# A state-space layer and a mixture of experts in one program: channel sums by column tiles of TensorE, and other ranks for the chain ahead of the next chunk's scan

## The chip, the cores and the metric

The kernel runs on one NeuronCore of a Trainium2 chip, in fp32. The metric is the device time of one execution in microseconds (us); lower is better. The core has five engines with a queue each: TensorE (PE, matmul; its weight loads are shown as PEld), VectorE (DVE), ScalarE (ACT), GpSimd (POOL) and SyncE (SP), whose queue issues nearly all of the DMAs here. Each queue is worked off in the order in which the kernel issued it.

## The reference

The input x has 8 images of 384 channels and 32 x 32 pixels; a sequence has 1024 tokens. Two layers follow each other, each added to its own input.

```python
# layer 0, on _gn(x): a selective state-space block
mu = t.mean(-1, keepdims=True); var = t.var(-1, keepdims=True)         # over the 384 channels
t = (t - mu) * rsqrt(var + 1e-05) * ln_w + ln_b
xm, z = split(t @ in_proj_w.T)                                         # 768 channels each
xc = silu(conv over 3 tokens (xm) + conv_b)
dt, Bm, Cm = split(xc @ x_proj_w.T, [24, 24 + 16])                     # 768 -> 56 channels
dt = softplus(dt @ dt_proj_w.T + dt_proj_b)
hst = exp(dt * A) * hst + dt * xc * Bm;  y = sum_n hst * Cm            # a scan over tokens, 16 states
t = ((y + xc * D) * silu(z)) @ out_proj_w.T
t = gelu(t @ mlp_w1.T + mlp_b1) @ mlp_w2.T + mlp_b2
# layer 1, on _gn(x): 4 experts, the two best weighted for each pixel
```

`_gn` is a group norm in 32 groups of 12 channels. The two products that the change is about are the means over 384 channels (mean and variance) and `xc @ x_proj_w.T`.

## The kernel before

**Tiling.** Channels lie on the 128 partitions, tokens on the free axis. A chunk is 512 tokens of one image (`NCH` = 16 chunks); the 384 channels make `J` = 3 tiles, the 768 inner channels `ND` = 6. The 16 states stand as 4 on the partitions and `NG` = 4 groups. A chunk so has 6 x 4 = 24 **rounds**, one for each inner tile and group, 384 in all.

**A round** (the main loop from L1008) is written out by hand: the sum over states of the last round (`sum_states`, four 32-column products y, L776), two pairs of scans on VectorE (L750), the drive of the next round on GpSimd (du, L742, 128x2048), the decays on ScalarE (da_A and da_B, L734), and the product with C, half on VectorE and half on GpSimd (L754). The tiles are few: three du, one da_A, one da_B, one y.

**The side work** is done between these. It is a set of Python generators (tasks); each yields before a step the engine that it needs, the planner's cost in us, and a least wait in slots. A round has three slots (`side`), in each of which TensorE gets 2.7 us of credit, VectorE 0.6 and ScalarE 2.7, 1.8 or 0.7. `issue` takes the tasks in order of urgency, which is

```python
return self.rank * PATIENCE + self.ready
```

with `PATIENCE` = 6 slots, so a lower rank goes first. The default rank is 2. "bank" stands for TensorE with a PSUM bank out of four (`ps_g`), "batch" for a SiLU or GELU batch that brings its own table loads on ScalarE. `plan(i, k)` says which tasks begin in round k of chunk i: `gate`, `conv` and `silus` for the next chunk n = i + 1, then `x_proj(n)` at k = 11, `delta(n, 0)` and `delta(n, 1)` at k = 17 and 21, `norm(n + 1)` at k = 21. Four lanes run throughout: output projection, hidden MLP layer, second MLP layer, and the first expert layer, which keeps up with the chunks. All this is settled when the program is built, so the order on each engine is fixed.

**What the change touches.** `norm` computes the mean of the three channel tiles as three products with a full 128x128 matrix of 1/384, accumulated in one PSUM bank mu (L266), so that each partition holds the mean; VectorE subtracts it (L268); ScalarE squares (sq, L275); three more products give var (L279), followed by Ln and Exp (L281, L283), a VectorE product (L285) and the affine step (L289). The weights of the mean carry the group norm's scale (mean_w, L253). `x_proj` accumulates six products with 56 columns in g_x (L360), one for each inner tile as its SiLU is done, and ScalarE copies the 56 rows to dbc (L365). Its B and C rows go to DRAM and come back spread over partitions (L368, L373). `delta` makes dt from dbc: product g_dt (L398), three ScalarE steps (L402 to L406), VectorE (L408), then dtx = dt * xc on GpSimd (L411), DMAs of both to DRAM and back, repeated over partitions (L384, L390). `statistics` reads x in parts (L241) for the group norm, from SP's queue, in a buffer of its own (`pst`). `seed` starts y with the skip term D * xc; the very first one is a product with the matrix skip (L767).

The router's logits already have the form that the change gives to the others: three 32-column products side by side (L577), a copy (L581), products that add the parts (L584).

After the scans come the last chunk's projections and MLP, the remaining expert hidden products (L622), the routing, and the second expert layer (L944).

Of the kernel before, what the change touches and what calls it, by code (L numbers as in the profile page):

```python
# [11 lines left out]
F32 = mybir.dt.float32  # L12
AF = mybir.ActivationFunctionType
ALU = mybir.AluOpType
# [4 lines left out]
P = 128  # L19
# [91 lines left out]
def layers(ctx, tc, io, ident, cmean, eps, dram, x1_dram, gn1, logits, r_dram, group_norm):  # L111
# [9 lines left out]
    def pool(name, bufs, stack=ctx, **kw):  # L121
# [7 lines left out]
                              for name, bufs in (("p1", 1), ("pdt", 2), ("pxt", NH), ("pdu", 3), ("psq", 2)))  # L129
    pz, pxc, ph, pbc, pst = (pool(name, bufs, scanning)  # L130
                             for name, bufs in (("pz", ND), ("pxc", 2 * ND), ("ph", HID), ("pbc", NG), ("pst", 1)))
# [23 lines left out]
    w_x = weight("x_proj", [P, ND, DTR + 2 * NS])  # L155
# [11 lines left out]
    V.tensor_reduce(sum_j, ident[0:32 * J, 0:32 * J].rearrange("p (j m) -> p m j", j=J)[:, 0:E, :], AX.X, ALU.add)  # L167
    e_b1 = weight("e_b1", [P, E * J])
# [12 lines left out]
    skip = wp.tile([P, P], F32, name="skip")  # L181
    V.tensor_scalar(skip, ident, d_skip[:, 0:1], None, ALU.mult)
# [49 lines left out]
    def statistics(b):  # L232
        st = p2.tile([P, NH * J, 6], F32, name="st")
        for k in range(NH):
            for j in range(J):
                if b == 0:
                    part = xt[k][:, j, :]
                else:
                    yield "-", 0, 3
                    part = pst.tile([P, T], F32, name="part")  # L240
# [11 lines left out]
        mean_w = p1.tile([P, P], F32, name="mean_w")  # L252
        S.activation(mean_w, cmean, AF.Identity, scale=g[:, 0:1])  # L253
        S.activation(g[:, 1:2], small[:, 0:1], AF.Identity, bias=g[:, 1:2], scale=-float(J))
        free()
        gn[b] = g, mean_w

    def norm(i):
# [4 lines left out]
        yield "bank", 3, 0  # L263
        mu = bank("mu")
        for j in range(J):
            PE.matmul(mu, lhsT=mean_w, rhs=x[:, j, :], start=(j == 0), stop=(j == J - 1))  # L266
# [3 lines left out]
        sq, var = [], None  # L270
        for j in range(J + 1):
            if j < J:
                yield "ACT", 0.65, 2 * (j == 0)
                sq.append(psq.tile([P, T], F32, name="sq"))
                S.activation(sq[j], x[:, j, :], AF.Square, bias=g[:, 1:2])  # L275
            if j > 0:
                yield "PE" if var else "bank", 1, 1
                var = var or bank("var")
                PE.matmul(var, lhsT=cmean, rhs=sq[j - 1], start=(j == 1), stop=(j == J))  # L279
# [72 lines left out]
    def x_proj(i):  # L352
        g = None
        m = DTR + 2 * NS
        for d in range(ND):
            while (i, d) not in xc:
                yield "-", 0, 1
            yield "bank" if d == 0 else "PE", 1, 1 if d % 3 == 0 else 0
            g = bank("g_x") if d == 0 else g
            PE.matmul(g[0:m, :], lhsT=w_x[:, d, :], rhs=xc[i, d], start=(d == 0), stop=(d == ND - 1))  # L360
# [724 lines left out]
```

## Time and profile before

| | |
|---|---|
| Median of 3 runs | 3993.1 us (3990.06 to 3995.06) |
| Profiled execution | 3992.75 us |
| Its span, first to last instruction | 3990.6 us, mean granted TensorE clock 0.96 |
| First scan, last round's first scan | 77.2 us, 3296.4 us from the start |
| Mean round | 8.4 us |
| TensorE busy | 3663.8 us (92%) |
| GpSimd, VectorE, ScalarE busy | 2776.9, 3031.7, 2421.2 us |
| mu (L266), var (L279), g_x (L360): busy | 47.6, 53.4, 91.7 us |

All views come from the one profiled execution. A line of a group or timeline gives the source line, the engine, the operation, what it writes and reads, and how many there are; an fp32 matmul stands as two records. A line of the waits view reads "engine, line waited for: us in total, times, longest". The timeline gives start, length, and in brackets the idle time of the engine before it and what ended it. Matmuls are pipelined, so their length is longer than what they occupy: the start of the next tells that.

### The profile page before, as it was taken

How to read it: one execution, taken by the hardware profiler on the slowest of the kernel's cores; microseconds unless marked ns; L12 is line 12 of the kernel's file. 1: busy time of each engine (PE TensorE's matmuls, PEld its weight loads, DVE VectorE, ACT ScalarE, POOL GpSimd, SP SyncE). 2: the span in 40 equal slices, each digit the busy share in tenths (PEclk: the TensorE clock that was granted, in tenths of full speed). 3: DMA queues.
4: the chain of work that ended last, by engine and by line, in shares of the span. 5: the costliest groups of instructions: out<-in, count | busy, mean ns of one | idle time of the engine just before them, and what ended most of it. 6: DMA issues, size and time to landing. Idle time of an engine off the chain costs nothing.

```text
span 3990.6 us, 35138 instructions
## 1 busy us (share of the span) xinstructions
PE 3663.8 (92%) x10294; PEld 1381.3 (35%) x10294; DVE 3031.7 (76%) x3081; ACT 2421.2 (61%) x3762; POOL 2776.9 (70%) x1070
## 2 busy tenths in 40 slices
PE   6679898899999999999999999999999889899999
PEld 2213233333333333333333333333333334344444
DVE  3898999888888887788888887888787881255554
ACT  4658677767687768676777777777767663200000
POOL 2898999788888888788878888888788880000000
PEclk8879899999999999999999999999999999999999
DMA  4344444465545454555455454555554443555553
GB/s 131 128 143 147 157 147 163 138 206 171 177 147 194 164 186 141 199 175 183 156 171 200 162 173 152 196 173 169 165 181 163 163 161 101 205 210 182 194 188 106
DMA packets 372499, 665.31 MB, mean 167 GB/s; under 512 B 40252, under 2 KB 151228, under 8 KB 370132
## 3 DMA queue, kind: packets, MB, share of 16 engines
q1 hardware_dynamic: 342496, 612.38, 46.2%
q10 hardware_dynamic: 29812, 50.68, 3.4%
q8 instruction: 83, 1.36, 0.1%
q14 instruction: 108, 0.88, 0.1%
HBM read 535.90 MB, written 127.01 MB: 166 GB/s over the span
## 4 chain that ended last, share of the span: by engine, by line
PE 51%; ACT 24%; DVE 13%; DMA 5%; issue 4%; POOL 2%; SPq 1%; ACTq 0%; DVEq 0%; POOLq 0%
PE acc L944 12%; PE acc L521 7%; PE e_hid L622 6%; PE hid L482 6%; PE g_in L297 5%; PE g_out L460 5%; ACT da_A L734 5%; PE y L776 5%; DVE da_A L750 4%; DVE du L750 4%; ACT da_B L734 3%; ACT L193 2%; PE g_dt L398 2%; ACT h L497 2%; DVE du L754 1%
## 5 line engine op out<-in xcount | busy, mean ns | idle before, releaser
L742 POOL TENSOR_TENSOR du<-dxr,b 128x2048 f32<-128x2048 f32 x384 | 1739.0, 4529 | 33.6 <-PE y L776 22.0
L754 POOL TENSOR_TENSOR du<-du,c 128x1024 f32<-128x1024 f32 x384 | 905.6, 2358 | 146.3 <-DVE du L750 127.4
L734 ACT ACTIVATE da_B<-dtr_b,w_a_log 128x512 f32<-128x512 f32 x768 | 527.3, 687 | 358.8 <-DVE du L750 321.6
L734 ACT ACTIVATE da_A<-dtr_a,w_a_log 128x512 f32<-128x512 f32 x768 | 528.3, 688 | 268.8 <-DVE carry L759 126.5
L776 PE MATMUL y<-du,sel 128*32 128x512 f32 x3072 | 467.1, 634 | 133.1 <-DVE du L754 65.3
L297 PE MATMUL g_in<-xt,in_proj 128*128 128x512 f32 x1152 | 566.6, 631 | 19.9 <-ACT edge L314 5.6
L482 PE MATMUL hid<-tt,mlp_w 128*128 128x512 f32 x1152 | 536.7, 609 | 45.9 <-ACT h L486 45.5
L750 DVE TENSOR_TENSOR_SCAN du<-da_B,carry,du 128x512 f32<-128x512 f32 x384 | 488.4, 1272 | 94.9 <-ACT da_B L734 93.5
L521 PE MATMUL acc<-h,mlp_w 128*128 128x512 f32 x1152 | 532.5, 605 | 19.3 <-ACT h L497 6.8
L750 DVE TENSOR_TENSOR_SCAN du<-da_B,du 128x512 f32<-128x512 f32 x384 | 465.0, 1211 | 95.2 <-ACT da_B L734 72.7
L622 PE MATMUL e_hid<-xn,e_w 128*128 128x512 f32 x1080 | 504.9, 615 | 26.9 <-ACT r L626 11.0
L750 DVE TENSOR_TENSOR_SCAN da_A<-da_A,carry,du 128x512 f32<-128x512 f32 x384 | 490.2, 1277 | 36.0 <-ACT da_A L734 35.9
L944 PE MATMUL acc<-r,w_e_w 128*128 128x512 f32 x1152 | 494.6, 592 | 0.0
L750 DVE TENSOR_TENSOR_SCAN da_A<-da_A,du 128x512 f32<-128x512 f32 x384 | 466.4, 1215 | 25.3 <-ACT da_A L734 23.5
L754 DVE TENSOR_TENSOR du<-da_A,c 128x1024 f32<-128x1024 f32 x384 | 470.3, 1225 | 13.2
L297 PEld LDWEIGHTS g_in<-xt,in_proj 128*128 128x128 f32 x1152 | 214.1, 197 | 369.9 <-issue 266.7
L482 PEld LDWEIGHTS hid<-tt,mlp_w 128*128 128x128 f32 x1152 | 218.0, 193 | 340.9 <-issue 254.3
L521 PEld LDWEIGHTS acc<-h,mlp_w 128*128 128x128 f32 x1152 | 214.5, 192 | 327.2 <-issue 253.8
L944 PEld LDWEIGHTS acc<-r,w_e_w 128*128 128x128 f32 x1152 | 218.9, 190 | 275.5 <-issue 275.5
L622 PEld LDWEIGHTS e_hid<-xn,e_w 128*128 128x128 f32 x1080 | 204.4, 195 | 316.5 <-issue 247.3
L411 POOL TENSOR_TENSOR dtx<-dt,xc 128x512 f32<-128x512 f32 x96 | 121.9, 1269 | 271.9 <-DVE dt L408 256.4
L460 PE MATMUL g_out<-xc,out_proj 128*128 128x512 f32 x576 | 271.6, 620 | 14.8 <-DVE xc L783 11.0
(129 smaller groups left out, 3021.3 us busy)
## 6 DMA issues: line engine op xcount, KB each, us to landing
dxr<-dxr_dram SPq DMA_DIRECT2D x384, 256.0 KB, 4.6
mlp_w<-in_mlp_w SPq DMA_DIRECT2D x384, 192.0 KB, 2.7
dtr_b<-dtr_dram SPq DMA_DIRECT2D x192, 256.0 KB, 4.2
dtr_a<-dtr_dram SPq DMA_DIRECT2D x192, 256.0 KB, 3.2
r_dram<-r ACTq DMA_DIRECT2D x192, 256.0 KB, 3.3
r<-r_dram SPq DMA_DIRECT2D x64, 768.0 KB, 4.6
in_proj<-in_in_proj SPq DMA_DIRECT2D x192, 192.0 KB, 3.5
e_w<-in_e_w SPq DMA_DIRECT2D x192, 192.0 KB, 2.6
```

The lines of the kernel that those rows point to most:

```text
L297: PE.matmul(g, lhsT=w[:, j, :], rhs=xt[i][:, j, :], start=(j == 0), stop=(j == J - 1))
L411: G.tensor_tensor(dtx, dt, xc[i, d], ALU.mult)
L460: PE.matmul(g, lhsT=w[:, d, :], rhs=xc[i, 3 * k + d], start=(k + d == 0), stop=(k == 1 and d == 2))
L482: PE.matmul(g, lhsT=w[:, j, :], rhs=tt[i][:, j, :], start=(j == 0), stop=(j == J - 1))
L521: PE.matmul(g, lhsT=w[:, n, :], rhs=hs[mine[n]], start=(k + n == 0), stop=(k == 1 and n == 2))
L622: PE.matmul(h, lhsT=w[:, j, :], rhs=xn[:, j, :], start=(j == 0), stop=(j == J - 1))
L734: S.activation(out, dtr[i, d][pair][:, j % 2, :], AF.Exp, scale=neg_a[:, d, j, s:s + 1])
L742: G.tensor_tensor(du[r], dxr[i, d], wide(bt[i, s].unsqueeze(1), [P, Q, T]), ALU.mult)
L750: V.tensor_tensor_scan(a if j < 2 else b, a, b, start, ALU.mult, ALU.add)
L754: engine.tensor_tensor(du[r][:, js, :], h, wide(ct[i, s].unsqueeze(1), [P, 2, T]), ALU.mult)
L776: PE.matmul(y[j * m:(j + 1) * m, :], lhsT=sel, rhs=h[:, j, :], start=False, stop=(s == NG - 1), tile_position=(0, j * m), skip_group_check ...
L944: PE.matmul(acc[j], lhsT=e2[:, e, d, j, :], rhs=r[:, d, :], start=(e + d == 0), stop=(e + d == E + J - 2))
```

## The change

Mean and variance: each of the three channel tiles goes to its own 32 columns of TensorE (`tile_position`) and so to its own 32 partitions of the PSUM bank. ScalarE copies these 96 rows into a psq tile, and one product with a 96x128 matrix of 1/32 adds them and spreads the sum over all partitions, into the same bank. The variance's products come after all three squares, not one after each. `x_proj`: the weights are padded with zeros to 64 columns, two inner tiles go side by side, three times; ScalarE copies the 128 rows, and one product with a matrix of two stacked unit matrices adds the halves. The parts for `statistics`, the copies and skip share the pool psq with the squares (three buffers in place of two, and `pst` is gone). Ranks: `conv` 2 to 1, the SiLU of xc and `x_proj` 2 to 0, `norm` 2 to 1 and begun at k = 18 in place of 21. Planner's costs follow.

```diff
-                              for name, bufs in (("p1", 1), ("pdt", 2), ("pxt", NH), ("pdu", 3), ("psq", 2)))
+                              for name, bufs in (("p1", 1), ("pdt", 2), ("pxt", NH), ("pdu", 3), ("psq", 3)))
...
-    w_x = weight("x_proj", [P, ND, DTR + 2 * NS])
+    w_x = wp.tile([P, ND, 64], F32, name="w_x_proj")
+    G.memset(w_x, 0.0)
+    S.dma_start(w_x[:, :, 0:DTR + 2 * NS], io["x_proj"])
+    sum_x = wp.tile([P, DTR + 2 * NS], F32, name="sum_x")
+    V.tensor_tensor(sum_x, ident[:, 0:DTR + 2 * NS], ident[:, 64:64 + DTR + 2 * NS], ALU.add)
...
+    spread = wp.tile([32 * J, P], F32, name="spread_j")
+    G.memset(spread, 1.0 / 32)
...
-                    part = pst.tile([P, T], F32, name="part")
+                    part = psq.tile([P, T], F32, name="sq")
...
-        mean_w = p1.tile([P, P], F32, name="mean_w")
-        S.activation(mean_w, cmean, AF.Identity, scale=g[:, 0:1])
+        mean_w = p1.tile([P, 32], F32, name="mean_w")
+        S.activation(mean_w, cmean[:, 0:32], AF.Identity, scale=g[:, 0:1])
...
+    def over_channels(out, weights, parts):
+        for j in range(J):
+            PE.matmul(out[32 * j:32 * (j + 1), :], lhsT=weights, rhs=parts[j], start=True, stop=True,
+                      tile_position=(0, 32 * j))
+        yield "ACT", 0.6, 2
+        rows = psq.tile([P, T], F32, name="sq")[0:32 * J, :]
+        S.copy(rows, out[0:32 * J, :])
+        yield "PE", 1, 2
+        PE.matmul(out, lhsT=spread, rhs=rows, start=True, stop=True)
...
-        yield "bank", 3, 0
+        yield "bank", 1.2, 0
         mu = bank("mu")
-        for j in range(J):
-            PE.matmul(mu, lhsT=mean_w, rhs=x[:, j, :], start=(j == 0), stop=(j == J - 1))
+        yield from over_channels(mu, mean_w, [x[:, j, :] for j in range(J)])
...
-        sq, var = [], None
-        for j in range(J + 1):
-            if j < J:
-                yield "ACT", 0.65, 2 * (j == 0)
-                sq.append(psq.tile([P, T], F32, name="sq"))
-                S.activation(sq[j], x[:, j, :], AF.Square, bias=g[:, 1:2])
-            if j > 0:
-                yield "PE" if var else "bank", 1, 1
-                var = var or bank("var")
-                PE.matmul(var, lhsT=cmean, rhs=sq[j - 1], start=(j == 1), stop=(j == J))
+        sq = []
+        for j in range(J):
+            yield "ACT", 0.65, 2 * (j == 0)
+            sq.append(psq.tile([P, T], F32, name="sq"))
+            S.activation(sq[j], x[:, j, :], AF.Square, bias=g[:, 1:2])
+        yield "bank", 1.2, 2
+        var = bank("var")
+        yield from over_channels(var, cmean[:, 0:32], sq)
...
-        for d in range(ND):
-            while (i, d) not in xc:
+        for d in range(0, ND, 2):
+            while (i, d) not in xc or (i, d + 1) not in xc:
                 yield "-", 0, 1
-            yield "bank" if d == 0 else "PE", 1, 1 if d % 3 == 0 else 0
-            g = bank("g_x") if d == 0 else g
-            PE.matmul(g[0:m, :], lhsT=w_x[:, d, :], rhs=xc[i, d], start=(d == 0), stop=(d == ND - 1))
+            yield "bank" if d == 0 else "PE", 1.1, 1 if d != 2 else 0
+            if d == 0:
+                g = bank("g_x")
+            for k in range(2):
+                PE.matmul(g[64 * k:64 * (k + 1), :], lhsT=w_x[:, d + k, :], rhs=xc[i, d + k], start=(d == 0),
+                          stop=(d == ND - 2), tile_position=(0, 64 * k))
+        yield "ACT", 0.6, 2
+        halves = psq.tile([P, T], F32, name="sq")
+        S.copy(halves, g)
+        yield "PE", 1, 2
+        PE.matmul(g[0:m, :], lhsT=sum_x, rhs=halves, start=True, stop=True)
...
+            skip = psq.tile([P, T], F32, name="sq")[:, 0:P]
+            V.tensor_scalar(skip, ident, d_skip[:, 0:1], None, ALU.mult)
             PE.matmul(y, lhsT=skip, rhs=xc[i, d], start=True, stop=True)
...
-                begin(conv(n, k - 5))
+                begin(conv(n, k - 5), rank=1)
             if k in (7, 10):
-                begin(silus(xc, accs, [(n, k - 7 + d) for d in range(3)]))
+                begin(silus(xc, accs, [(n, k - 7 + d) for d in range(3)]), rank=0)
...
-                begin(x_proj(n))
+                begin(x_proj(n), rank=0)
...
-        if k == 21 and n + 1 < NCH:
-            begin(norm(n + 1))
+        if k == 18 and n + 1 < NCH:
+            begin(norm(n + 1), rank=1)
```

More of the change, by code (lines that the diff above doesn't have):

```diff
@@ L128, in layers @@
     p1, pdt, pxt, pdu, psq = (pool(name, bufs, scanning)
-                              for name, bufs in (("p1", 1), ("pdt", 2), ("pxt", NH), ("pdu", 3), ("psq", 2)))
-    pz, pxc, ph, pbc, pst = (pool(name, bufs, scanning)
-                             for name, bufs in (("pz", ND), ("pxc", 2 * ND), ("ph", HID), ("pbc", NG), ("pst", 1)))
+                              for name, bufs in (("p1", 1), ("pdt", 2), ("pxt", NH), ("pdu", 3), ("psq", 3)))
+    pz, pxc, ph, pbc = (pool(name, bufs, scanning)
+                             for name, bufs in (("pz", ND), ("pxc", 2 * ND), ("ph", HID), ("pbc", NG)))
     pw_in, pw_out, pw_1, pw_2 = (pool("pw_" + name, 3, scanning) for name in ("in", "out", "1", "2"))
@@ L180, in layers @@
     V.tensor_reduce(sel, ident.rearrange("p (m k) -> p m k", k=Q), AX.X, ALU.add)
-    skip = wp.tile([P, P], F32, name="skip")
-    V.tensor_scalar(skip, ident, d_skip[:, 0:1], None, ALU.mult)
     edge0 = wp.tile([P, ND, 2], F32, name="edge0")
@@ L352, in x_proj @@
     def x_proj(i):
-        g = None
         m = DTR + 2 * NS
-        for d in range(ND):
-            while (i, d) not in xc:
+        for d in range(0, ND, 2):
+            while (i, d) not in xc or (i, d + 1) not in xc:
                 yield "-", 0, 1
-            yield "bank" if d == 0 else "PE", 1, 1 if d % 3 == 0 else 0
-            g = bank("g_x") if d == 0 else g
-            PE.matmul(g[0:m, :], lhsT=w_x[:, d, :], rhs=xc[i, d], start=(d == 0), stop=(d == ND - 1))
+            yield "bank" if d == 0 else "PE", 1.1, 1 if d != 2 else 0
[9 more added lines that the diff above has]
+        PE.matmul(g[0:m, :], lhsT=sum_x, rhs=halves, start=True, stop=True)
         yield "ACT", 0.6, 2
```

## The prediction

> **What bounds the kernel now.** I read the page's busy table first, then the busy time by stage, then the waits, and last the timeline of TensorE, because a busy matmul row does not say what a product really occupies.
>
> ```profile
> span 3990.6 us, 35138 instructions
> ## 1 busy us (share of the span) xinstructions
> PE 3663.8 (92%) x10294; PEld 1381.3 (35%) x10294; DVE 3031.7 (76%) x3081; ACT 2421.2 (61%) x3762; POOL 2776.9 (70%) x1070
> ```
>
> TensorE leads by far. The next view has one stage per row; I cut at the first scan of chunks 0, 2, 4, 5 and 8, and at the end of the scans. Columns: stage, its length, then PE, PEld, DVE, ACT, POOL busy, granted clock, DMA.
>
> ```profile
> 77.19:264.30 187.11, 124.98 (x312) 32.78 (x314) 166.83 (x178) 119.41 (x186) 173.78 (x78) 0.73 0.41 135
> ...
> 455.90:644.30 188.40, 170.12 (x486) 58.54 (x486) 170.89 (x188) 137.31 (x210) 174.41 (x79) 0.93 0.48 159
> ...
> 852.50:1056.80 204.30, 195.52 (x579) 73.03 (x578) 172.15 (x189) 148.23 (x227) 175.92 (x79) 0.98 0.56 186
> 1056.80:1266.20 209.40, 196.14 (x574) 72.18 (x573) 171.57 (x157) 154.24 (x245) 170.01 (x54) 0.97 0.48 158
> ...
> 1682.70:1883.90 201.20, 192.29 (x575) 71.65 (x574) 171.96 (x188) 148.60 (x227) 175.78 (x79) 0.99 0.57 190
> ...
> 3305.00:3990.60 685.60, 662.50 (x1553) 291.46 (x1551) 287.04 (x351) 60.07 (x90) 0.69 (x2) 0.99 0.48 169
> ```
>
> From chunk 3 on a chunk takes 201 to 214 us and TensorE is busy for some 194 of it; VectorE (172), GpSimd (170 to 176) and ScalarE (148 to 154) have 30 us and more to spare. Chunks 0 to 2 lack the expert products, take 187 to 192 us, and are held by the scan's own chain, with GpSimd at 92%. In a steady chunk GpSimd needs 4.53 + 2.36 us a round for the drive and the half read-out, about 7.0 with the rest, so 24 rounds are 168 us at least; the chunk is 205 because TensorE has more to do than that. What spoils TensorE's last 10 us is here:
>
> ```profile
> POOL dtx L411 <- DVE dt L408: 256.4, 81, 58.0
> ...
> PE y L776 <- DVE du L754: 65.3, 32, 4.9
> ...
> PE hid L482 <- ACT h L486: 45.5, 23, 4.8
> ...
> PE var L279 <- ACT sq L275: 15.4, 11, 4.1
> ```
>
> The first row is the weak spot of the scan: every fourth round GpSimd stands before dtx until the step size dt has come through TensorE, three ScalarE steps and VectorE. A fuller TensorE queue makes it later. The last row is the variance product waiting for its squares one at a time.
>
> TensorE's timeline shows what a product occupies, from its start to the start of the next:
>
> ```profile
> 1657.12 1.07 PE L776 MATMUL y<-du,sel 128*32 128x512 f32 x8
> 1658.12 1.12 PE L398 MATMUL g_dt<-dbc,w_dt_proj 24*128 24x512 f32 x2
> 1659.17 2.84 PE L266 MATMUL mu<-xt,mean_w 128*128 128x512 f32 x6
> 1661.85 2.74 PE L521 MATMUL acc<-h,mlp_w 128*128 128x512 f32 x6
> ...
> 2011.56 1.06 PE L577 MATMUL g_logits<-x,w_gate_w 128*32 128x512 f32 x6 [0.36 <-ACT h L486]
> 2012.55 1.92 PE L360 MATMUL g_x<-xc,w_x_proj 128*56 128x512 f32 x4
> ```
>
> Each product stands as two records. Three full products (mu) hold TensorE for 2.68 us; one alone (g_dt) 1.05; four 32-column products side by side (y) 1.00; three of them (g_logits) 0.99. So the kernel already has the changed form, and its price.
>
> **What the Trainium skill says.** "TensorE: Matmul & The Clock Gate", section Measured speedup vs the span model, gives 2.38 times for three 32-column products at 512 columns; this trace gives more, 2.68 / 0.99 = 2.7. "TensorEngine Tiling (Array Packing)", Key Properties, says that changing the tiling mode drains TensorE. The trace bounds that: where g_logits stands right ahead of y the two take 1.85 us together (1520.34 to 1522.19), 0.93 each, against 1.00 and 0.99 alone, so a switch is some 0.1 us. The same page, PSUM Bottleneck, warns that tiling does not speed up the evacuation; here it adds ScalarE copies, priced below. The clock gate page (What's actually happening) has the clock halve after an idle window; the trace agrees in kind, 0.73 granted in chunk 0 and 0.97 to 0.99 in full chunks.
>
> **The change part by part.**
>
> *Mean and variance* (16 times each). Removed: three full products, 2.68 us. Added: three side by side, 0.99, and one product that adds and spreads, between 0.90 (a third of 2.71, three g_x products in a row) and 1.05 (g_dt): I take 0.95. Saved 0.74 each, 1.48 a chunk.
>
> *x_proj* (16 times). Removed: six products, 2 x 2.71 = 5.42. Added: three pairs of 64 columns and one sum. No pair of this width is in the trace: between 0.90 (a product's own time) and 1.80 (no overlap); I take 0.99, the column group's price. 5.42 - 2.97 - 0.95 = 1.50 a chunk; with no overlap it would be a loss of 0.9.
>
> Together 2.98 us of TensorE a chunk, 48 in all, with ends of 10 (no overlap of pairs) and 53.
>
> *Three copies a chunk* on ScalarE: the like copy of g_logits takes 0.57, so 1.7 a chunk, 28 in all. ScalarE idles some 50 us of a chunk, which hides them; without that cover they would cost those 28. Behind each stands a TensorE product, a new wait. In the built order of the changed kernel at least a y group of the next round, and mostly two to four groups of three products, stand between the column products and that product, 3 to 10 us, against 0.57 of copy: I take 0. The nearest wait, hid on h, is 45.5 / 23 = 2.0 us; on 48 waits 95 us is the bad end.
>
> *Variance after all squares.* The 15.4 us of waits go, as all three squares are issued before the column products. I count two thirds, 10, since TensorE is the bound where most of them lie.
>
> *Buffers.* The parts for the statistics share three psq buffers with squares and copies. In the built order their loads lose the wait on the last part's statistics and nothing late is ahead of them: 0. Zeroing w_x on GpSimd delays its load; it is needed at 50.5 us: 0. skip moves to just before the first y: under 1 us, once.
>
> *Ranks.* The convolution, its SiLU batches and x_proj go ahead of evictions. In the built order of an ordinary chunk the second half of x_proj ends in round 15 or 16 as before 16, the first dt of the next chunk comes in round 17 instead of 18 to 19, and the mean of every second chunk in round 18 instead of 21. Its bc write, dtr and dxr writes and their repeats move up SP's queue by as much, past weight loads; TensorE waits for weights 4 us in all now, and two tiles are loaded ahead: 0. The trace shows no wait of the next chunk's first rounds for this chain (rounds 0 and 23 take 7.4 us from scan to scan), so being earlier earns nothing there: 0. Both ends are open: the third rival.
>
> *Ahead of the scans* all stands in series: norm and x_proj of chunk 0 trade 2 to 3 us of products for three copies and the turns between engines. I put +2.
>
> *What of the 48 comes through.* Adding each round's products at the prices above and taking the larger of that and 7.0 us, a round at a time, yields only 14 of 45; letting TensorE's backlog carry over one round yields all. The du buffers (three) and PSUM banks (four) allow about a round. I take 75% in the eleven full chunks with both parts and chunk 14, which has x_proj alone: 0.75 x (11 x 2.98 + 1.5) = 26; half of 10.4 (three times 2.98 and the norm of chunk 1, which is also done there) in chunks 0 to 2: 5. The scan-free end has the same order: 0.
>
> Sum: -26 - 5 - 10 + 2 = -39, say -38. The profiled execution took 3992.75 us (span 3990.6 and 2.15 around it), the median is 3993.1; I predict **3955**.
>
> **The rivals.**
>
> *Rounds swallow it* (20%). The floor of 7.0 us and the dt wait bind round by round; 14 comes through, less the 2 ahead of the scans and nothing for the squares: 3981. For it: rounds of chunk 0 to 2 gain nothing from an idle TensorE. Against: 194 of 205 us busy.
>
> *Reordering adds to it* (10%). dt is no longer late behind a full queue: a quarter of the 256 us before dtx goes on top of 10 to 20 us: 3920 to 3935. For it: that row is the longest of GpSimd's. Against: the dt order in the other rounds is the same.
>
> *The rank change makes dt later* (15%). Convolution steps, SiLU batches (1.28 + 3 x 0.56 + 1.28 us with their table loads) and the new copies stand before the dt steps on ScalarE; VectorE's dt and GpSimd's dtx, with the next drive behind it, come later. In the built order the dtx of rounds 1 and 21 slips in half the chunks into the next round. There are some 90 of them: the gain is gone at 0.42 us each, slower by 0.2% at 0.5 us; one wait as now (256.4 / 81 = 3.2 us) on 16 of the slipped ones is 51, so 4006, and pairs without overlap would add 38 x 0.75.
>
> That the change does not do what it says is the pairs' part: with no overlap TensorE is relieved by 10 us, and with the squares' 10 and the +2 the result is about 3977, beside the first rival.
>
> **How the numbers follow.** Main case 55%, its own range 3935 to 3972. A measurement of this kernel can tell 0.2%, 8 us, from no change. Faster: 55 + 10 and 13 of the first rival's 20; within: 7; slower: 15. The range 3922 to 4000 reaches the first rival whole, most of the second, and the near part of the third.
>
> **What would show it.** mu and var at 0.99 + 0.95 us start to start; the pairs of g_x near 1.0 us each; PE's busy sum lower by 40 to 55; no wait of the two adding products on a copy over a few us in all; the row of var on sq gone; steady chunks of 202 us, the end unchanged. I am wrong if pairs take 1.8, if POOL's wait before dtx grows by over 40 us, or if PE's busy time falls by its 48 while chunks stay at 205.

## The result, and the profile after

The changed kernel takes **4038.1 us** (median of 5 runs, 4034.43 to 4042.35), the kernel before 3992.1 beside it: ratio 1.012 with a 95% interval of 1.0106 to 1.0135. It is 46 us slower, where 38 faster was predicted. Its profiled execution took 4039.29 us. The page's head and busy table after:

```profile
span 4037.6 us, 35369 instructions
...
PE 3653.5 (90%) x10390; PEld 1360.4 (34%) x10390; DVE 3038.4 (75%) x3082; ACT 2444.8 (61%) x3810; POOL 2781.3 (69%) x1072
```

TensorE's busy time is only 10 us lower, and the span is 47 longer. The first scan starts at 79.4 us (77.2 before), the last round's first scan at 3343.5 (3296.4), and what follows takes 694.1 us (694.2). So all but 2 us of the loss lies between the scans. The same stages as before, cut at this kernel's own chunk starts (columns: stage, length, then PE, PEld, DVE, ACT, POOL busy, granted clock, DMA):

```profile
...
857.40:1069.30 211.90, 196.96 (x571) 72.23 (x569) 172.31 (x189) 147.44 (x226) 177.25 (x80) 0.96 0.54 178
1069.30:1276.50 207.20, 189.75 (x584) 69.02 (x585) 172.95 (x158) 157.57 (x250) 170.41 (x54) 0.97 0.49 162
1693.20:1903.30 210.10, 193.90 (x571) 70.97 (x569) 172.02 (x188) 147.26 (x226) 177.21 (x80) 0.98 0.54 180
3352.00:4037.60 685.60, 663.05 (x1553) 291.35 (x1551) 287.12 (x351) 60.09 (x90) 0.74 (x2) 0.98 0.48 169
```

Chunk 4 (first row) is 212 us instead of 204, chunk 5 (second) 207 instead of 209, chunk 8 (third) 210 instead of 201; the end (last row) is unchanged. TensorE's busy share of chunk 8 is 92% instead of 96%. Taken from scan start to scan start, the even chunks 4 to 14 are 8.3 us longer on average and the odd chunks 3 to 13 1.8 shorter. In the even chunks rounds 13 and 14 are the largest part, +3.6 and +5.2.

The products themselves are as cheap as forecast. TensorE's timeline (start, length, product, and in brackets the idle time before it):

```profile
1823.18 1.08 PE L374 MATMUL g_x<-xc,w_x_proj 128*64 128x512 f32 x4
1824.19 2.84 PE L541 MATMUL acc<-h,mlp_w 128*128 128x512 f32 x6
...
2061.46 1.03 PE L266 MATMUL mu<-xt,mean_w 128*32 128x512 f32 x6
2067.19 4.54 PE L642 MATMUL e_hid<-xn,e_w 128*128 128x512 f32 x6 [4.69 <-ACT r L646]
...
2077.91 1.02 PE L272 MATMUL mu<-sq,spread_j 96*128 96x512 f32 x2
2078.77 2.74 PE L642 MATMUL e_hid<-xn,e_w 128*128 128x512 f32 x6
```

A pair of g_x occupies 1.01 us from its start to the next, the spread product 0.86; three columns of mu or var have 0.99 where a product follows at once. The second group shows where such a saving can go: mu ends, and e_hid stands idle for 4.69 us until ScalarE has evicted r.

The waits, those that answer to the rows of before first (engine, line waited for: us in total, times, longest):

```profile
POOL dtx L431 <- DVE dt L428: 258.7, 78, 58.4
PE y L798 <- DVE du L774: 87.9, 39, 7.0
...
PE e_hid L642 <- ACT r L646: 28.4, 7, 4.7
...
PE var L266 <- ACT sq L289: 18.6, 8, 3.2
PE g_in L310 <- ACT r L646: 16.9, 6, 2.8
PE g_in L310 <- DVE x L546: 13.9, 6, 2.4
```

and the same rows of before that were not shown yet:

```profile
PE e_hid L622 <- ACT r L626: 11.0, 4, 2.9
...
PE g_in L297 <- DVE x L526: 2.9, 3, 1.1
PE g_in L297 <- ACT r L626: 2.1, 3, 0.7
```

GpSimd's wait before dtx, the weak spot of the prediction, is unchanged in sum. New are TensorE's waits for a PSUM bank: e_hid on r 28.4 against 11.0, g_in on r 16.9 against 2.1, g_in on x 13.9 against 2.9, together +43, and y on du +23. One of them in full, round 12 and 13 of chunk 8, TensorE after:

```profile
1798.19 2.84 PE L541 MATMUL acc<-h,mlp_w 128*128 128x512 f32 x6 [1.50 <-ACT h L517]
1803.43 4.29 PE L310 MATMUL g_in<-xt,in_proj 128*128 128x512 f32 x6 [2.39 <-DVE x L546]
...
1811.47 1.12 PE L418 MATMUL g_dt<-dbc,w_dt_proj 24*128 24x512 f32 x2
1815.41 4.27 PE L310 MATMUL g_in<-xt,in_proj 128*128 128x512 f32 x6 [2.82 <-ACT r L646]
```

and GpSimd beside it:

```profile
1815.64 1.27 POOL L431 TENSOR_TENSOR dtx<-dt,xc 128x512 f32<-128x512 f32 x1 [6.90 <-DVE dt L428]
```

The second half of an MLP product (acc) stands first and waits for its GELU batch on ScalarE. The next g_in takes acc's bank, and VectorE's eviction of that bank comes late: 2.39 us. g_in itself then takes 4.29 us in place of 2.84. Then come e_hid and y (left out); y, and g_dt behind it, are late by all of this, and GpSimd stands 6.90 us before dtx. Round 13 takes 14.0 us in place of 9.8. The long g_in is the clock; the window of it (same columns as above):

```profile
1804.70:1808.10 3.40, 3.40 (x5) 1.33 (x4) 3.23 (x3) 0.79 (x2) 2.33 (x3) 0.50 0.00 0
```

After two waits TensorE runs 3.4 us at a granted clock of 0.50, with a granted clock of 1.00 in the four us on either side. "TensorE: Matmul & The Clock Gate", section A second HAM failure mode: psum-queue depth-cycling, of the Trainium skill describes such a case, in bf16: short idle moments between groups of matmuls that cycle through PSUM banks make the clock swing between half and full. This trace agrees. By the clock records the half-clock time between the first and the last scan is 363 us, 288 before, and each of its 53 spells follows 3.4 us in which TensorE stood idle for 1.0 us or more, 2.3 in the median; of the 827 other such stretches at full clock, 42 have over 1.0. At half clock the records of a full product start 0.85 us apart and not 0.43, so half of the time in which TensorE works at it is lost. TensorE works in 265 us of the 363 and in 225 of the 288; in the rest it stands idle, which the gaps count already.

This gives an account of the stretch between the scans. TensorE's work at full clock is its busy time less half of the busy time at half clock; its losses are its gaps over 0.1 us plus that half.

| Between the scans, us | Length | Work at full clock | Gaps | Half of busy time at half clock |
|---|---|---|---|---|
| before | 3219 | 2834 | 281 | 112 |
| after | 3264 | 2802 | 333 | 133 |
| difference | +45 | -32 | +52 | +20 |

(Gaps under 0.1 us make up the other 5.) The forecast gives the changed products some 45 us less between the scans; their own rows fall from 163 to 125 us, by 38, and all of TensorE's work by 32. Waits and half clock add 72. The experiments ask which part of the change brought them.

### The profile page after: what moved, and what is told of

The parts are those of the page before. It is cut to its first block, busy times and chain, and to the rows that moved or that the text cites. A ratio compares the mean times of both kernels' runs of the same rounds, so it can differ in the third digit from the quotient of the medians.

```text
span 4037.6 us, 35369 instructions
## 1 busy us (share of the span) xinstructions
PE 3653.5 (90%) x10390; PEld 1360.4 (34%) x10390; DVE 3038.4 (75%) x3082; ACT 2444.8 (61%) x3810; POOL 2781.3 (69%) x1072
## 4 chain that ended last, share of the span: by engine, by line
PE 60%; ACT 20%; DVE 11%; issue 3%; DMA 3%; POOL 2%; SPq 1%; ACTq 0%; POOLq 0%; DVEq 0%
PE acc L966 12%; PE acc L541 10%; PE e_hid L642 9%; PE g_in L310 7%; PE hid L502 6%; PE g_out L480 6%; PE y L798 5%; ACT da_A L754 4%; DVE du L770 3%; ACT da_B L754 3%; DVE da_A L770 3%; PE g_dt L418 2%; ACT L199 2%; DVE du L774 1%; ACT h L517 1%
## 5 line engine op out<-in xcount | busy, mean ns | idle before, releaser
L310 PE MATMUL g_in<-xt,in_proj 128*128 128x512 f32 x1152 | 580.0, 645 | 54.3 <-ACT r L646 16.9
L541 PE MATMUL acc<-h,mlp_w 128*128 128x512 f32 x1152 | 539.1, 612 | 34.2 <-ACT h L506 16.9
L642 PE MATMUL e_hid<-xn,e_w 128*128 128x512 f32 x1080 | 506.0, 614 | 44.1 <-ACT r L646 28.4
L431 POOL TENSOR_TENSOR dtx<-dt,xc 128x512 f32<-128x512 f32 x96 | 121.8, 1269 | 263.8 <-DVE dt L428 258.7
```

What stands on the lines that cost most here:

```text
L310: PE.matmul(g, lhsT=w[:, j, :], rhs=xt[i][:, j, :], start=(j == 0), stop=(j == J - 1))
L431: G.tensor_tensor(dtx, dt, xc[i, d], ALU.mult)
L541: PE.matmul(g, lhsT=w[:, n, :], rhs=hs[mine[n]], start=(k + n == 0), stop=(k == 1 and n == 2))
L642: PE.matmul(h, lhsT=w[:, j, :], rhs=xn[:, j, :], start=(j == 0), stop=(j == J - 1))
```

## The experiments

Ratios are to the kernel before, run beside it (medians 3988 to 3997 us), with the 95% interval. Shifts of single chunks and rounds are taken from the starts of the scans in the profiled execution, against before.

**1. The packing in the old order.** Changed kernel, but all of before's planner steps, costs and ranks are kept; the copies and adding products stand in added steps of no cost, with a least wait of one slot.

```diff
-        yield "ACT", 0.6, 2
+        yield "-", 0, 1
         rows = psq.tile([P, T], F32, name="sq")[0:32 * J, :]
         S.copy(rows, out[0:32 * J, :])
-        yield "PE", 1, 2
+        yield "-", 0, 1
         PE.matmul(out, lhsT=spread, rhs=rows, start=True, stop=True)
```

> The packed products, copies and adding products of the change, in the order of instructions of the kernel before: the planner sees the old steps, costs and ranks, and the copy and the adding product are put in without cost. Theory A (the loss is one of order: what the ranks and the new steps do to the side work): this order has no long rounds 13 and 14, so the relieved TensorE shows as a gain, 10 to 35 us below the kernel before, about 3965. Theory B (the packed form itself costs, by its copies, waits and mode switches): 30 to 50 us above before, about 4030, as the change.

Measured: 4047.7, ratio 1.0149 (1.0134 to 1.0165). The old order does not bring the saving: theory A falls, and theory B is the nearer one. Part of the reason is the copy, which here has no cover:

```profile
PE mu L272 <- ACT sq L270: 15.7, 10, 2.3
PE var L272 <- ACT sq L270: 13.9, 12, 2.2
```

30 us of waits on copies, where the changed kernel has 1.5 in these rows: the two slots of planned wait around the copy are worth something. The rest is spread: chunk 0 (+14.7) and round 17 of the odd chunks (+3.4 each) have most of it. Work at full clock falls to 2791, but gaps and half-clock losses rise by 90, with no rank changed.

**2. The changed order without the packing.** The changed kernel's planner steps, with full products in place of the column products; copies and adding products are left out.

```diff
-            PE.matmul(out[32 * j:32 * (j + 1), :], lhsT=weights, rhs=parts[j], start=True, stop=True,
-                      tile_position=(0, 32 * j))
+            PE.matmul(out, lhsT=weights, rhs=parts[j], start=(j == 0), stop=(j == J - 1))
```

> The order, ranks and planner's costs of the changed kernel, but with the old full products for mean, variance and x_proj in the same places; the copies and the adding products are left out. Theory A (order): slower still than the change, by what packing is worth in this order, 0 to 30 us: 4040 to 4070. Theory B (packing itself costs): back near the kernel before, 3985 to 4000.

Measured: 4067.2, ratio 1.02 (1.0185 to 1.0215). So in this order the packed products save 29 to 32 us (by medians and by ratios), near the 31 that the prediction took for them, and the order costs 75 to 80.

```profile
PE e_hid L631 <- ACT r L635: 16.9, 7, 2.8
```

This wait is 28.4 with the packing. In round 19 of the odd chunks ScalarE has a SiLU batch with its table loads between e_hid and r, and TensorE has only mu to do meanwhile: 1.7 us shorter, it makes the wait as much longer, 7 x 1.7 = 12 us. A part of the saving is handed back there.

**3. The ranks without the packing.** The kernel before with the four rank changes.

```diff
-                begin(conv(n, k - 5))
+                begin(conv(n, k - 5), rank=1)
...
-                begin(silus(xc, accs, [(n, k - 7 + d) for d in range(3)]))
+                begin(silus(xc, accs, [(n, k - 7 + d) for d in range(3)]), rank=0)
...
-                begin(x_proj(n))
+                begin(x_proj(n), rank=0)
...
-        if k == 21 and n + 1 < NCH:
-            begin(norm(n + 1))
+        if k == 18 and n + 1 < NCH:
+            begin(norm(n + 1), rank=1)
```

> The kernel before with the four changes of ranks and of norm's begin, nothing else. Theory A with the ranks as the cause of the order: the pair of slow rounds 13 and 14 in chunks 4, 6, ... 14 appears, and the time is 30 to 60 us above before, 4020 to 4050. Theory B: within 10 us of before.

Measured: 4038.9, ratio 1.0131 (1.0116 to 1.0146). The edit that the prediction put at 0 costs some 50 us, and work at full clock is unchanged (2837, 2834 before). The changed kernel, with the same ranks, takes 4038.1: beside these ranks its packing, with the planner steps that it needs, brings nothing. Even chunks are 14.7 longer, odd ones 7.4 shorter; rounds 13 and 14 are late as in the changed kernel (+2.4 and +3.8), and round 0 is late in a new way:

```profile
1677.80 5.42 PE L622 MATMUL e_hid<-xn,e_w 128*128 128x512 f32 x12
1686.45 4.36 PE L622 MATMUL e_hid<-xn,e_w 128*128 128x512 f32 x6 [3.23 <-DMA e_w<-in_e_w]
```

and its waits:

```profile
PE e_hid L622 <- DMA e_w<-in_e_w: 20.1, 6, 3.7
...
PE g_out L460 <- DMA out_proj<-in_out_proj: 14.9, 6, 3.0
```

With the norm's products gone ahead, five expert products in a row each want a new weight tile; before, var's products stood between them. Read from the timelines, that gave the loads time, and most of the 35 us of waits on weights here come from its loss, where the prediction said "TensorE waits for weights 4 us in all now, and two tiles are loaded ahead: 0".

**4. acc a slot later.** Changed kernel, one planned slot more before acc.

```diff
-                yield "bank" if k == 0 else "PE", 3, 1 if j == 0 else 0
+                yield "bank" if k == 0 else "PE", 3, 2 if j == 0 else 0
```

> The changed kernel with one number changed: the second MLP layer's first product of a half waits two slots after its GELU, not one, so that in rounds 12 of the even chunks it no longer stands ahead of its GELU and of the gate's product. Theory A, in the form that these rounds hold the loss (TensorE stands behind a bank whose eviction is planned a third later, and g_dt behind it): rounds 13 and 14 of even chunks fall from 14.0 and 13 us to under 10, and 40 us or more of the loss go: 3975 to 4005. If the loss is spread over the order: 4025 to 4045. Theory B: 4030 to 4045.

Measured: 4058.4, ratio 1.0179 (1.0162 to 1.0196). acc no longer leads round 12, but g_in then waits 4.5 us on average for another bank, evicted by ScalarE (r) behind a GELU batch; round 13 still takes 12 to 16 us. The position of acc is not the cause.

**5 and 6. A fifth bank for the side work.** da_B goes from PSUM to SBUF and gives its bank to `ps_g`; in the order of before, and in that of experiment 3.

```diff
-    ps_g = pool("ps_g", BANKS, space=PSUM)
+    ps_g = pool("ps_g", BANKS + 1, space=PSUM)
...
-    ps_a, ps_b, ps_y = (pool("ps_" + name, 1, scanning, space=PSUM) for name in "aby")
+    ps_a, ps_y = (pool("ps_" + name, 1, scanning, space=PSUM) for name in "ay")
+    ps_b = pool("sb_b", 1, scanning)
```

> The kernel before, instruction for instruction in the same order, with a fifth PSUM bank for the side work (da_B moves to SBUF to make room, the statistics' parts share the squares' buffers, the last layer has three spare banks for four). The planner still stops at four held banks. Theory C (TensorE stands behind banks whose eviction is planned a third or more later, its clock halves, and y and g_dt behind it come late): some of the 122 us of bank waits of before goes: 3940 to 3980. Theory D (the order of TensorE's work as such, not the banks): within 12 us of before.

> e3 (before with the change's ranks alone) in its same order, with the same fifth bank as e5. Theory C: with the bank waits gone the loss of e3 goes too: within 15 us of e5. Theory D: it stays 35 to 55 us above e5.

Measured: 4784.7, ratio 1.1981 (1.1951 to 1.2012), and 4771.0, ratio 1.1952 (1.1915 to 1.1988). The attempt failed by what it had to move. Groups of VectorE, experiment 5 (line, operation, shapes, times | busy us, mean ns | idle before):

```profile
L751 DVE TENSOR_TENSOR_SCAN du<-da_B,carry,du 128x512 f32<-128x512 f32 x384 | 1057.5, 2754 | 33.6 <-ACT da_B L735 33.5
...
L751 DVE TENSOR_TENSOR_SCAN da_A<-da_A,carry,du 128x512 f32<-128x512 f32 x384 | 487.4, 1269 | 15.7 <-ACT da_A L735 15.7
```

and the first of them before:

```profile
L750 DVE TENSOR_TENSOR_SCAN du<-da_B,carry,du 128x512 f32<-128x512 f32 x384 | 488.4, 1272 | 94.9 <-ACT da_B L734 93.5 <-POOL du L742 1.3
```

A scan with da_B in SBUF takes 2.75 us on average, with it in PSUM 1.27; da_A, still in PSUM, is unchanged in the same run. The trace of experiment 5 tells why:

```profile
2005.74 5.48 POOL L743 TENSOR_TENSOR du<-dxr,b 128x2048 f32<-128x2048 f32 x1
2008.41 3.89 DVE L751 TENSOR_TENSOR_SCAN du<-da_B,carry,du 128x512 f32<-128x512 f32 x1
```

The drive on GpSimd ends at 2011.22, the scan 1.08 us later. All 368 scans on da_B that begin while a drive runs end so, 1.08 us behind it; they take 4.3 us on average. The 192 that no GpSimd instruction overlaps take 1.22. So it is not a slower scan, but one that waits for the drive to end. VectorE's busy share becomes the largest (87%, TensorE 82%). The question of the banks is not answered; but here, where TensorE is not the busiest engine, the ranks cost nothing (-14).

**7. x_proj begun only when all six xc are there**, so that g_x holds its bank for two rounds in place of five. Changed kernel otherwise.

```diff
-        for d in range(0, ND, 2):
-            while (i, d) not in xc or (i, d + 1) not in xc:
-                yield "-", 0, 1
+        while not all((i, d) in xc for d in range(ND)):
+            yield "-", 0, 1
+        for d in range(0, ND, 2):
```

> The changed kernel, but x_proj begins only when all six inner tiles have their SiLU, so that its bank is held for some two rounds and not from round 11 to 16. Theory C: rounds 13 and 14 of even chunks, where three banks do the side work of four, lose their stall: 3995 to 4020. Theory D: as the change, 4030 to 4050.

Measured: 4028.4, ratio 1.0077 (1.0046 to 1.0107). Rounds 13 and 14 of even chunks are back at the level of before (-1.1 and -0.2), so the bank that g_x holds is what they lack. But 10 to 17 us (by medians and by ratios) is all that comes of it: other rounds grow, with weights late in two places (acc on mlp_w 12.8 us, and):

```profile
PE e_hid L642 <- DMA e_w<-in_e_w: 17.1, 4, 5.0
```

**8. Only the norm's rank.** Changed kernel with `conv`, `silus` of xc and `x_proj` back at rank 2.

```diff
-                begin(conv(n, k - 5), rank=1)
+                begin(conv(n, k - 5))
...
-                begin(x_proj(n), rank=0)
+                begin(x_proj(n))
```

> The changed kernel with conv, the SiLU of xc and x_proj back at rank 2; only norm keeps its rank 1 and its begin in round 18. If the ranks of the chain cause the loss: 3985 to 4010. If the loss comes from the packed form's steps in the planner or from norm's place: 4030 to 4050. Theory C says only that the time goes with the bank waits and the low clock in its trace.

Measured: 4052.3, ratio 1.0146 (1.0115 to 1.0178). Undoing those three ranks brings nothing back, so in the packed kernel they are not what costs. The time lies just above the range given for the packed steps or the norm's place.

**9. Mean and variance alone, old ranks.** The changed kernel's norm; x_proj, all ranks and the norm's start as before. Against the changed kernel, beside the old `x_proj`:

```diff
-        if k == 18 and n + 1 < NCH:
-            begin(norm(n + 1), rank=1)
+        if k == 21 and n + 1 < NCH:
+            begin(norm(n + 1))
```

> Mean and variance by column tiles with copy and spread product, x_proj and all ranks and starts as in the kernel before (norm at rank 2, k = 21); the planner draws the order anew from the new costs. Theory E (every newly drawn order costs 40 to 80 us beside that of before, whatever it was drawn for): 16 chunks x 1.48 us of TensorE x 0.75 = 18 saved, against 40 to 80: 4015 to 4055. Theory R (the earlier ranks are what costs): 18 saved and nothing lost, 3970 to 3985.

Measured: **3980.2**, ratio 0.9965 (0.9952 to 0.9979), 12 to 14 us faster than before, in theory R's range (but see experiment 10). The variance's waits did go here:

```profile
PE var L262 <- ACT sq L285: 3.5, 2, 2.7
```

Theory E, that any newly drawn order costs 40 us or more, falls.

**10. Another order, nothing else.** Before with one number of the planner changed.

```diff
-PATIENCE = 6
+PATIENCE = 7
```

> The kernel before with PATIENCE = 7 slots a rank in place of 6: no product, copy or rank changes, only the order in which the planner takes ready tasks. Theory E: 4010 to 4060, since before's order is a rare good one. Theory R: within 0.4% of before, 3977 to 4008, with gains and losses from chunk to chunk that cancel.

Measured: 3979.5, ratio 0.9976 (0.9963 to 0.9988). Chunks move by -4.6 to +3.2 and nearly cancel (the traced execution is the longest of the 20, 3998.7). This order, drawn anew for no purpose, is worth 10 us; gains of that size in the rows here may be chance of the order. The order of before is no rare find.

**11. The norm one round earlier.** Before with the norm at k = 20, rank unchanged.

```diff
-        if k == 21 and n + 1 < NCH:
+        if k == 20 and n + 1 < NCH:
```

> The kernel before with norm(n + 1) begun at k = 20 in place of 21, rank unchanged: a small shift, about a fifth of the TensorE rows in another place that the rank change moves. Theory E, in its strong form, 4005 to 4040; if the cost goes with how much of the order moves, 3995 to 4010. Theory R: 3985 to 4000.

Measured: 4002.2, ratio 1.0019 (1.0011 to 1.0028). The cost appears where experiment 3 had it: rounds 0 and 1 of even chunks +2.8 and +2.6, TensorE waiting 12.2 us for e_w.

**12. The ranks of conv, SiLU and x_proj alone**, in the kernel before: the first three edits of experiment 3, without the fourth.

> The kernel before with the ranks of conv (1), SiLU of xc (0) and x_proj (0) alone; norm stays at rank 2 and k = 21. All four together cost 50 us. Theory R1 (the norm's early start is the costly part, since it falls into the rounds with the second half of the expert's products): 3985 to 4005. Theory R2 (the SiLU and convolution ahead of bank evictions are the costly part): 4025 to 4045. Theory E: 4010 to 4060, with the losses in other rounds than 13 and 14.

Measured: 3990.7, ratio 0.999 (0.998 to 1.0). Rounds 13 and 14 of even chunks are 3.2 and 3.5 longer, with the waits of g_in on r (16.9) and x (13.4) as in the changed kernel; the odd chunks gain 6.6 and the even ones lose 5.7. So the stall that the trace shows best is bought back elsewhere, and is not the net cost.

**13. The norm's rank and start alone**, in the kernel before: the fourth edit of experiment 3, without the first three.

> The kernel before with the norm's part of the rank change alone (rank 1, begun at k = 18 in place of 21). Theory N (the early norm is the costly part): all four ranks cost 50, the other three -2, so 4030 to 4045, with TensorE waiting for expert and projection weights in rounds 22 to 1 of even chunks. Rival S (the two parts cost only together, since each alone still leaves slack): 3990 to 4012.

Measured: 4002.3, ratio 1.0029 (1.0017 to 1.0041): +11, not the 45 of theory N. Experiments 12 and 13 add up to 9, both together (experiment 3) cost some 50. The two parts interact, as rival S said. With the same ranks and both packings, experiment 8 took 4052.3: there the packing costs some 50.

**14. The norm's start undone in the changed kernel** (rank 1 kept).

```diff
-        if k == 18 and n + 1 < NCH:
+        if k == 21 and n + 1 < NCH:
             begin(norm(n + 1), rank=1)
```

> The changed kernel with norm(n + 1) begun at k = 21 again (rank 1 kept: the norm is late for the chunk otherwise); all else as changed. Theory N: the norm's start costs 40 to 50 of the changed kernel, so 3985 to 4000, and with the whole of the packing (29) beside the ranks of conv, SiLU and x_proj (0) at best 3961. Rival S: 4020 to 4040, since round 13 and 14 of even chunks, where the trace shows most of the loss, come long before the norm's start.

Measured: 4071.5, ratio 1.0196 (1.016 to 1.0232): worse than the changed kernel by 30 to 33, outside both expectations. Gaps are 360 us, the largest but for the runs with a fifth bank. Theory N in its simple form falls.

**15. x_proj alone, its ranks, norm late.** Mean and variance as full products with rank and start as before; x_proj and the ranks as changed:

```diff
+            for k in range(2):
+                PE.matmul(g[64 * k:64 * (k + 1), :], lhsT=w_x[:, d + k, :], rhs=xc[i, d + k], start=(d == 0),
+                          stop=(d == ND - 2), tile_position=(0, 64 * k))
```

> x_proj by two column tiles with copy and sum, and the ranks of conv (1), SiLU (0) and x_proj (0); mean and variance as full products at rank 2 and k = 21 as before. Theory N: 12 chunks x 1.50 x 0.75 = 13 saved, ranks free: 3972 to 3985. Rival S: even chunks longer by the g_in and acc waits of rounds 13 and 14 without the odd chunks gaining: 4000 to 4030.

Measured: 3982.6, ratio 0.9982 (0.9972 to 0.9992). The waits of rounds 13 and 14 are there (+3.5, +4.3) and the odd chunks gain 7.1:

```profile
PE g_in L301 <- ACT r L637: 16.9, 6, 2.8
```

With 14.0 on x, these are the changed kernel's waits to a tenth, in a kernel that is faster than before. Against this kernel, the changed one differs by nothing in rounds 6 to 13 and 15 to 21 of the even chunks, and is 60 us longer in all: the early, packed norm loses them mostly in rounds 0 to 7 (even chunks: +2.9, -2.0, +1.9 in rounds 0 to 2; odd chunks: +2.0, +1.4, +2.8 in rounds 3 to 5).

**16 and 17. Both packings, norm late, shorter planned waits.** The norm's longer chain has to begin early because of its least waits of two slots; with one slot each it can begin at rank 2 and k = 21 (16) or 20 (17).

```diff
-        yield "ACT", 0.6, 2
+        yield "ACT", 0.6, 1
         rows = psq.tile([P, T], F32, name="sq")[0:32 * J, :]
         S.copy(rows, out[0:32 * J, :])
-        yield "PE", 1, 2
+        yield "PE", 1, 1
...
-        if k == 18 and n + 1 < NCH:
-            begin(norm(n + 1), rank=1)
+        if k == 21 and n + 1 < NCH:
+            begin(norm(n + 1))
```

> The changed kernel with norm(n + 1) at rank 2 and k = 21 as before, made possible by least waits of one slot in place of two in the norm's chain (copy, adding product, subtraction, variance, Ln); conv, SiLU and x_proj keep the changed ranks. Theory C (the early norm on top of the other ranks is what loses): e15's 3983 less the 12 of the norm's packing: 3965 to 3985. Rival X (the packings disturb each other, through the three shared psq buffers and the denser queue): 4010 to 4045. If the waits of one slot are too short, TensorE waits for mu's and var's copies: 32 x up to 1 us on top.

> As e16 with the norm begun at k = 20, rank 2: in the order on TensorE the closest of the versions with both packings to e15 (some 200 of 5000 products stand elsewhere, 350 in e16). Theory C: 3965 to 3990, the k = 20 start cost 10 in the kernel before. Rival X: 4010 to 4045.

Measured: 4019.2, ratio 1.0068 (1.0047 to 1.0089), and 4036.1, ratio 1.0115 (1.0091 to 1.0138). The first is 19 us better than the changed kernel and still 37 worse than x_proj alone; by the traces 34 of 40 lie in chunks 1 to 6, chunk 1 having 12.8. The short waits have their price, PE var on the copy 17.7 us. Rival X came true in its number. Its mechanism did not: for a free psq buffer no engine waits over a few us in sum, in the changed kernel or here.

**18. x_proj alone with the late start of experiment 7** (its diff, applied to experiment 15).

> e15 (x_proj alone by two column tiles, with its ranks, norm late) with x_proj begun only when all six xc are there, so that g_x holds its PSUM bank for two rounds in place of five. Theory B (the bank is what rounds 13 and 14 of the even chunks lack): 7.8 us in each of six even chunks come back, and the rest stays: 3983 - 47 = 3936, at least below 3965. Rival M (the work of these rounds is only moved, TensorE's sum stays): even chunks shorter in 13 and 14 and as much longer elsewhere, 3975 to 4000.

Measured: 3986.0, ratio 0.9986 (0.9976 to 0.9997). Rounds 13 and 14 of the even chunks are cured (-0.8 and -0.1), and so are the odd chunks' gains (-1.7 in place of -7.1). Rival M holds: this stall only moves work from one chunk to the next.

The runs side by side, each from its own trace:

| Kernel | Ratio | Work at full clock | Gaps + half of busy time at half clock |
|---|---|---|---|
| before | 1 | 2834 | 394 |
| ranks of conv, SiLU, x_proj (12) | 0.999 | 2837 | 384 |
| early norm (13) | 1.0029 | 2838 | 403 |
| all four ranks (3) | 1.0131 | 2837 | 433 |
| the change's order, nothing packed (2) | 1.02 | 2837 | 456 |
| mean and variance packed (9) | 0.9965 | 2802 | 408 |
| x_proj packed, its ranks (15) | 0.9982 | 2825 | 380 |
| both packed, order of before (1) | 1.0149 | 2791 | 484 |
| both packed, norm late (16) | 1.0068 | 2808 | 439 |
| after: both packed, all ranks | 1.012 | 2802 | 466 |

The five kernels with full products agree in the work column within 4 us, as they should. For packed ones it is good to some 15, since ends of matmuls are modelled: 9 and 15 should both save 22 between the scans, and on the rows of the changed products alone they save 24 and 21. The last column decides: it rises by 39 with the four ranks, by 90 with both packings in the old order, and by 59 when the norm's packing joins x_proj's even with the norm late.

## Why the prediction was wrong

**The prices of the packing: right.** They are met within 0.1 us a product, and the changed products' own rows fell by 38 us between the scans (45 forecast). Ahead of the scans +2 and the end unchanged are right as well.

**"Ranks ... 0": the first step that failed.** The text looked for someone who gains from an earlier chain, found none, and wrote 0. It did not price what is pushed back. Experiment 3 measures the same edit at some 50 us with nothing packed. Two groups of waits were seen: banks whose eviction on ScalarE or VectorE comes later than the next product wants them (experiments 12 and 15, there without net cost), and, with the norm early, expert and projection weights late at the turn of the chunk (35 us in experiment 3, 12 in experiment 11; the text read 4 for all weights, the rows of before sum to 5). The parts cost -2 and +11 alone and 50 together, so a sum over parts would not have found it either.

**"I take 75%": the second.** The same ranks with and without the packing, each with the planner steps that it needs, as ratios to before:

| Ranks | Nothing packed | Both packed |
|---|---|---|
| as before | 1 | 1.0149 (1, copies without cover) |
| the norm's alone | 1.0029 (13) | 1.0146 (8) |
| conv, SiLU and x_proj alone | 0.999 (12) | 1.0068 (16, shorter planned waits) |
| all four | 1.0131 (3) | 1.012 (the change) |

Only in the last row does the packing not lose, and there it brings about 0.1%. So of the miss of 84 us, some 50 are the ranks, put at 0, and the other 34 or so are the saving that did not come. Taken the other way round, the packing costs 59 in the old order and the ranks take 10 of it back: the two cannot be told apart by a sum. The 29 to 32 us of experiment 2 are what shorter products save when every instruction keeps its place; the copies and the new planner steps change the places.

**The clock: missing.** The sum knew busy time and waits. In the stretch shown, waits of 1.5 and 2.4 us on TensorE went ahead of 3.4 us of half clock; over the scans there were 75 us more of it, TensorE worked in 40 of them, and that cost 20. The gap of round 13 repeats in every even chunk; experiments 7 and 18 show that the bank held by g_x is what it lacks, and that curing it is not the same as gaining time.

**"Variance after all squares ... 10": not in this order.** The row is 18.6 us (15.4 before): TensorE reaches the columns before ScalarE has squared. It fell to 3.5 where the norm stood late (experiment 9).

**Copies: right for this kernel.** The three rows of adding products on copies are 0.7, 0.8 and 1.5 us. The cover that the prediction named is real: without it they were 30 (experiment 1) and with one slot in place of two 19 (experiment 16: 17.7 and 1.5).

**Buffers: right as far as seen.** No wait for a shared psq buffer carries anything in the trace; it was not tried alone.

**Where a shorter product only lengthens a wait.** Where TensorE is short of work beside a ScalarE batch, the saving is lost on the spot (12 us in round 19).

**The third rival** had the sign and the wrong place. dt was not made late by VectorE's or ScalarE's queue: GpSimd's row before dtx is unchanged (256.4 and 258.7). Its price of 3.2 us on 16 slipped chains and 4006 was too small too. Of the marks set, "PE's busy falls by its 48 while chunks stay at 205" was met in part: the work fell by 32 between the scans, the busy row of the whole run by only 10 (40 to 55 was the mark), since more products ran at half clock, and the chunks shown went to 207 to 212.

**What stays open.** Why the two packings, neither of which loses alone, lose against before in one kernel in all the eight orders tried (experiments 1, 4, 7, 8, 14, 16, 17 and the change itself) is not settled. Neither buffers, nor the norm's start, nor the stall of rounds 13 and 14 explains it alone; the loss stands in different rounds each time. That the half clock follows from the waits was read from the traces, not tried apart. A fifth bank could not be tried cleanly.

The best kernel is that of experiment 9, mean and variance packed with the old ranks: 0.35% faster than before. x_proj's packing with its ranks gains 0.18%. Since a new order alone gained 0.24% (experiment 10), neither gain is shown to come from the packing.

## What to carry to other kernels

Price an edit of the order by what it pushes back (evictions, weight loads, the next round's first product), not only by what it brings forward. In a kernel whose main engine is busy at 95%, take a saving and a re-ordering apart and measure each: here one saving with its own new order gained 0.35%, the re-ordering alone lost 1.3%, and all together lost 1.2%. An order drawn anew for no purpose moved the time by 0.24%, so a gain of that size needs more than one order to be believed. A stall that the trace shows plainly may be paid back elsewhere; only its removal tells.

## What the runs showed of the hardware

A scan on VectorE with both streamed inputs in SBUF took 2.75 us on average beside GpSimd's work, against 1.27 with one of them in PSUM (experiment 5). "SBUF — State Buffer", section Who interferes with whom, says that a VectorE instruction with two SBUF inputs contends with a GpSimd instruction that reads SBUF. The trace agrees: without GpSimd beside it such a scan took 1.22 us, and each of the 368 that began during GpSimd's drive ended 1.08 us after that drive. A whole kernel went from 3997 to 4785 us, in the main by one small tile's move.

The clock's halves are easy to overlook in a mean. At a mean granted clock of 0.96 the kernel before had 321 us of half clock, at 0.95 the changed one had 403: one point of the mean looks like rounding and is 80 us of half clock. In the changed kernel 39 of the 53 spells between the scans came without any TensorE gap of over 3.4 us in the 3.4 us ahead of them; shorter gaps were enough.
